# Laying the early pair products of a graph layer ahead of the last gather group, with 45 more behind the third group

## The chip, the cores and the metric

The kernel runs on one core of a Trainium2 chip. The metric is the device time of one execution in microseconds (us). Engines are called as in the profile: PE (matmul) and PEld (its weight load), DVE (vector), ACT (scalar), POOL (GpSimd, here mostly the issuer of row gathers) and SP (issues transfers).

## What is computed

Four graph attention layers over one graph of N = 3,327 nodes with 256 features, each followed by the residual and a layer norm. The adjacency is symmetric, about 1% full, with a full diagonal.

```python
x = layernorm(x + L0(x, adj))   # scores a.leaky(W_s x_i + W_t x_j), softmax over neighbours, sums of W_t x_j
x = layernorm(x + L1(x, adj))   # scores leaky(s1_i + s2_j) of h = W x, softmax over neighbours, sums of h_j
x = layernorm(x + L2(x, adj))   # scores s_i + s_j + b (no leaky), softmax, sums of h_j
x = layernorm(x + L3(x, adj))   # two layers like L1 with 4 heads of 64, elu after each
```

In layer 1 the weight of a neighbour can be written exp(s1_i + s2_j) or its 0.2-fold, whichever is larger in the exponent. Factors of the row cancel in the softmax, so the kernel forms e = max(rate_i, f_j) x adjacency and multiplies by rows that already carry their own exponential. A partial sum over some column tiles j can be stored and the rest added later; a column of exponentials carried with the features gives the denominator. This is what makes "early products" possible.

## The kernel before

The nodes are 26 tiles of 128 rows. Layer 0 is *sparse* (`sparse0`): the rows are handled in four groups of `SETS = (4, 7, 9, 6)` tiles. For each group a *search* (`neighbours`, scan with MAX8 at L589, sort L597/L599, ranks L688/L692) lists each row's neighbours; POOL writes the lists (`write_list`, L741) and reads them back in order of length (`read_lists`, L749). Then 237 *parts*, each of up to four neighbours of the 128 rows of a tile, are gathered by POOL with one indirect transfer a neighbour (L926, g<-table_d), eight steps ahead of their use, in 22 buffers. DVE scores a part (`largest` L946, `weighted` L952); when a tile has all its scores, `weights` takes maximum and exponentials (L985, L990), and `combine` scales the rows on ACT (L1028) and sums them on PE against an identity (L1031). `add_input` divides and adds the input into a tile with the tag "hs" of two buffers (L1052 to L1058), and `put_back` stores it through POOL (L1065). The last tile's later cuts are summed on DVE instead (`add_aside`, L1007/L1009). When a group is complete, `take` loads it back into h, and `finish_sums`, `finish_root` (POOL, L1105) and `finish` (DVE, L1114) norm it.

All of this is one order written out by hand: in each step q, the loop at the end of `sparse0` first does so many steps of the next search as are owed by a due time (`owed`), then everything entered for this step by `at_step`, then the gather for part q + 8 and the score of part q. Engines keep this order. Parts of the groups begin at steps 0, 39, 102 and 182, and the last part is step 236. POOL's puts and list writes stand in a list `between` that is worked off between gathers.

Into the steps of layer 0 some work of layer 1 is laid. `load_next` loads its weight and two attention vectors, `dots_next` multiplies them (L1142, in tiles with the tag "hs" too). For the 20 tiles of the first three groups (`EARLY = 20`), `turn_next` and `project_next` make the layer 1 features and store them in `feats_d`. For the first two groups (`KNOWN = 11` tiles) the products of row tiles 0 to 10 with column tiles 0 to 10 are done early, too: for each *pair* of a trio of row tiles and a column tile, SP loads adjacency and features (at_f, three buffers), ACT casts the adjacency and stores it for a later layer (`weigh_early`, L1217), DVE forms e (L1221), PE adds (`add_early`, L1234), and after the last pair of a trio ACT copies the sums and stores them in `part_d` (`keep_early`, L1242). The trios are [0,1,2], [3,4], [5,6,7], [8,9,10], so there are 44 pairs.

Layer 1 itself (`one_head`) then goes over blocks of row tiles in the order 11 to 14, 0 to 4, 5 to 10, 15 to 19, 20 to 25. PE holds one accumulator for each row tile of the block and runs over the column tiles j (L1845), DVE forming e for each (L1728). Blocks of tiles up to 10 begin at j = 11 (`first_of`, `skip`) and add the stored sums by identity products (L1854) at j = skip + `LATER` (4). The preparation of the block before for layer 2 (turn L1765, copy, project L1653, bias L1691, scale L1692) lies in a queue `pending`; `work_off` takes steps of it, in these blocks once per column tile from j = skip + 4 on, and after the last column tile the rest. The end of group 3 (`last_group`) is worked off at the start of layer 1 in the same manner. Layers 2 and 3 follow in the same dense form; they are untouched.

Of the kernel before, what the change touches and what calls it, by code (L numbers as in the profile page):

```python
# [8 lines left out]
F32 = mybir.dt.float32  # L9
BF16 = mybir.dt.bfloat16  # L10
I32 = mybir.dt.int32
# [8 lines left out]
P = 128  # L20
# [12 lines left out]
SETS = (4, 7, 9, 6)  # L33
# [10 lines left out]
ROW = 260  # L44
# [6 lines left out]
def gat_stack(  # L51
# [29 lines left out]
    nc = tc.nc  # L81
    n, dim = x.shape
# [15 lines left out]
    ident = const.tile([P, P], F32, name="ident")  # L98
# [10 lines left out]
    EARLY = sum(SETS[:-1])  # L109
# [11 lines left out]
    KNOWN = sum(SETS[:-2])  # L121
    blocks1 = []
    for lo, hi in ((0, KNOWN), (KNOWN, EARLY), (EARLY, nt)):
        count = -(-(hi - lo) // 6)
# [6 lines left out]
    part_d = dram.tile([KNOWN * P, dim + 1], F32, name="part_d")  # L131
# [154 lines left out]


    def sparse0(lost):
        GROUP, TURNS, LEAD, SPREAD = 4, 22, 8, 8
        starts = [sum(SETS[:s]) for s in range(len(SETS))]  # L290
        with ExitStack() as s0:
            find = s0.enter_context(tc.tile_pool(name="s_find", bufs=2))
            const0 = s0.enter_context(tc.tile_pool(name="s_const", bufs=1))
            io0 = s0.enter_context(tc.tile_pool(name="s_io", bufs=2))
# [767 lines left out]
            def put_back(s, t):  # L1062

                entry = held.pop((s, t))
                nc.gpsimd.indirect_dma_start(  # L1065
                    out=sums_d[s][:, :],
                    out_offset=bass.IndirectOffsetOnAxis(
                        ap=entry["lst"][:, KMAX : KMAX + 1], axis=0
                    ),
                    in_=entry["y"][:, :], in_offset=None,  # L1070
                )
# [55 lines left out]
            def load_next():  # L1127
                nc.sync.dma_start(w1[:, :, :dim], l1_w_t.rearrange("(c p) f -> p c f", p=P))
                for v in (l1_a[dim:], l1_a[:dim]):
                    t = find.tile([P, dim], F32, tag="minus", name="row1")  # L1130
                    nc.sync.dma_start(
                        t, bass.AP(tensor=v.tensor, offset=v.offset, ap=[[0, P], [1, dim]])
                    )
                    rows1.append(t)

            def early_bank():
                return ps0.tile([P, BANK], F32, tag="v", name="early", bufs=4)
# [44 lines left out]
                for block in blocks1 if block[-1] < KNOWN  # L1182
                for lo in range(block[0], block[-1] + 1, 3)
            ]
            pairs1 = [(trio, j) for trio in trios for j in range(KNOWN)]
            asked1, formed1, state1 = {}, {}, {}

            def ask_early(m):
                if m >= len(pairs1):
                    return  # L1190
                trio, j = pairs1[m]
                lo, w = trio[0] * P, len(trio) * P
                if j == 0:
                    b = [trio[0] in block for block in blocks1].index(True)
                    at0 = trio[0] - blocks1[b][0]
                    rate = find.tile([P, 3 * P], F32, tag="adj_b", name="rate1", bufs=3)
                    rows = rate1_d[b][at0 : at0 + len(trio), :].rearrange("s i -> (s i)")
                    nc.sync.dma_start(rate[:, :w], rows[None].to_broadcast([P, w]))
                    state1["next"] = rate
                t = find.tile([P, PIECE], I32, tag="adj_i", name="at_f", bufs=3)  # L1200
                f = t[:, BANK : BANK + dim + 2].bitcast(F32)
                copy_rows(nc.sync, t[:, :w], adj_t[j * P : (j + 1) * P, lo : lo + w])
                nc.sync.dma_start(f, feats_d[j * P : (j + 1) * P, :])
                asked1[m] = t, f

            def weigh_early(m):
                trio, j = pairs1[m]
                lo, w = trio[0] * P, len(trio) * P
                t, f = asked1[m]
                if j == 0:  # L1210
                    state1["rate"] = state1["next"]
                if m == 0:
                    state1["e"] = find.tile(
                        [P, max(SETS) * P], F32, tag="key_rows", name="e1", bufs=1
                    )
                at = find.tile([P, 3 * P], BF16, tag="cand", name="at1")
                nc.scalar.copy(at[:, :w], t[:, :w])  # L1217
                nc.scalar.dma_start(at_d[j * P : (j + 1) * P, lo : lo + w], at[:, :w])
                x = m % 3 * 3 * P
                e = formed1[m] = state1["e"][:, x : x + w]  # L1220
                nc.vector.scalar_tensor_tensor(  # L1221
                    e, state1["rate"][:, :w], f[:, dim + 1 : dim + 2], t[:, :w],
                    op0=ALU.max, op1=ALU.mult,
                )

            def add_early(m):
                if m < 0:
                    return
                trio, j = pairs1[m]
                e, (_, f) = formed1.pop(m), asked1.pop(m)  # L1230
                if j == 0:
                    state1["accs"] = [early_bank() for _ in trio]
                for s, acc in enumerate(state1["accs"]):
                    nc.tensor.matmul(  # L1234
                        acc[:, : dim + 1], e[:, s * P : (s + 1) * P], f[:, : dim + 1],
                        start=(j == 0), stop=(j == KNOWN - 1),
                    )

            def keep_early(m):
# [47 lines left out]
            def at_step(q, what, *args):  # L1287
                due.setdefault(q, []).append(lambda: what(*args))
# [17 lines left out]
            for q, key in ends.items():  # L1306
                count = len(cuts_of(seats[key]))
                if key[1] == 0:
                    at_step(q + 2, send_weights, key[0])
                    at_step(q + 3, take_weights, key[0])  # L1310
                    at_step(q + 4, combine_excess, key[0])
                for i in range(count):
                    at_step(q + 1 + i * SPREAD // max(count, SPREAD), combine, *key, i)
                at_step(q + 10, add_input, *key)
                at_step(q + 13, between.append, lambda key=key: put_back(*key))
                if key[1] == SETS[key[0]] - 1 and key[0] < len(SETS) - 1:
                    at_step(q + 21, take, key[0])
                    at_step(q + 27, finish_sums, key[0])
                    at_step(q + 33, finish_root, key[0])
                    at_step(q + 37, finish, key[0])  # L1320
            for s, q in begins.items():
                work, at = excess(s), max(q - 2, 0)
                for y in range(12):
                    at_step(at + y, go_on, work)
            at = begins[len(SETS) - 1] - 2 * KNOWN - 3
            at_step(at - 12, load_next)
            at_step(at - 6, dots_next, 0)
            at_step(at - 4, dots_next, 1)
            for s in range(len(SETS) - 1):
                for it in range(starts[s], starts[s] + SETS[s]):  # L1330
                    at_step(at, turn_next, it)
                    at_step(at + 2, project_next, it)
                    at += 2
                if s == len(SETS) - 3:
                    at = max(at, begins[len(SETS) - 1] + 38)
            at = begins[len(SETS) - 1] + 2
            at_step(at - 2, ask_early, 0)
            at_step(at - 1, ask_early, 1)
            for m, (trio, j) in enumerate(pairs1):
                at_step(at, add_early, m - 1)  # L1340
                if j == 0 and m:
                    at_step(at + 1, keep_early, m - 1)
                    at += 1
                at_step(at, weigh_early, m)
                at_step(at, ask_early, m + 2)
                at += 1
            at_step(at, add_early, len(pairs1) - 1)
            at_step(at + 1, keep_early, len(pairs1) - 1)
            def keep_targets(s):
                lo, hi = starts[s] * P, min(n, (starts[s] + SETS[s]) * P)  # L1350
                copy_rows(nc.sync, own_d[s][: hi - lo, AT_TGT:], table_d[1 + lo : 1 + hi, :])
# [5 lines left out]
            ahead, owed, steps = [], {}, 0  # L1357
            for s in range(1, len(SETS)):
                at = begins[s] - LEAD - 2
                at_step(at, read_lists, s)  # L1360
                at -= SETS[s] // 2 + 1
                for it in range(SETS[s]):
                    at_step(at, between.append, lambda s=s, it=it: write_list(s, it))
                ahead.append(neighbours(s))
                steps += steps_of(s)
                owed[at] = steps
# [227 lines left out]
    def layers(rs, early=0, rest=None):  # L1594
# [209 lines left out]
                work_off()  # L1804

        def first_of(layer, b):
            return KNOWN if early and layer is l1 and layer.blocks[b][-1] < KNOWN else 0

        def ask_parts(block):

# [10 lines left out]
        def one_head(layer, make, banks_next):  # L1821
# [7 lines left out]
            for turn_b, b in enumerate(layer.order):  # L1829
# [6 lines left out]
                for j in range(skip, nt):  # L1836
# [3 lines left out]
                    for s, it in enumerate(block):  # L1840
                        pn = rows_of(it)
                        for part in range(1 if layer.leaky else 3):
# [6 lines left out]
                                start=(j == skip and part == 0),  # L1849
                                stop=(j == nt - 1 and (layer.leaky or part == 2)),  # L1850
                            )
                    if skip and j == skip + LATER:
                        for acc, y in zip(accs, parts):
                            nc.tensor.matmul(  # L1854
                                acc[:, : dim + 1], ident, y, start=False, stop=False
                            )
# [448 lines left out]
```

## Time and profile before

| | us |
|---|---|
| three timed runs | 3,307.76, 3,314.23, 3,329.03 (median 3,314.23) |
| profiled execution | 2,906.56 |
| its span | 2,904.8 (mean granted PE clock 0.887) |
| PE busy in the span | 2,310.4 (80%) |
| DVE busy | 2,128.0 (73%) |
| ACT busy | 866.0 (30%) |
| POOL busy | 991.7 (34%) |

The profiled execution is shorter than the timed runs; numbers from it are compared with its own time. In the page, a row of slices gives an engine's busy share in tenths over 40 equal slices of the span. A row of a group reads: line, engine, operation, output<-input, shapes, count | busy us, mean ns of one | idle us before, and who ended it. A row of the waits reads: engine, tile, line <- what it waited for: us in total, times, longest. A row of the timeline reads: start in us, duration, engine, line, operation, tiles and count, and in brackets the wait before it and what ended it.

### The profile page before, as it was taken

To read this page: it belongs to the slowest core of one execution; us is meant where nothing else is said; L and a number is where in the kernel's file an instruction comes from. 1 tells how busy PE (TensorE), PEld (TensorE's weight loads), DVE (VectorE), ACT (ScalarE), POOL (GpSimd) and SP (SyncE) were. 2 spreads that over 40 slices of the span, in tenths; PEclk is the share of its full clock that TensorE was granted. 3 is DMA by queue.
4 is the path that set the end of the run, shared out by engine and by line. 5 is a ranking of instruction groups with operands and counts; after the bars stand their busy time and mean duration, and the time that the engine had idled before them with its cause. 6 is when DMAs were issued, how large, how long until landed. Compare 5 with 4: busy or idle time off the path is not lost.

```text
span 2904.8 us, 47707 instructions
## 1 busy us (share of the span) xinstructions
PE 2310.4 (80%) x16735; PEld 1545.7 (53%) x16764; DVE 2128.0 (73%) x5634; ACT 866.0 (30%) x2441; POOL 991.7 (34%) x1059
## 2 busy tenths in 40 slices
PE   6466657555552665767899999999999999999997
PEld 4234435433442444645778888863656667534332
DVE  7799799968872856655455421158999999899997
ACT  4145445443432533544344311111011110110111
POOL 2676777777777777772000000000000000000000
PEclk9577778777776887889999999999999999999998
DMA  7795665445544557765767533331222222212211
GB/s 245 204 271 146 184 190 156 140 141 148 161 115 109 126 162 196 199 177 159 219 179 202 169 93 111 105 90 45 78 80 62 75 80 64 71 43 63 60 45 49
DMA packets 207558, 378.52 MB, mean 130 GB/s; under 512 B 38410, under 2 KB 148080, under 8 KB 206288
## 3 DMA queue, kind: packets, MB, share of 16 engines
q1 hardware_dynamic: 119416, 186.29, 22.5%
q0 software_dynamic: 50768, 154.31, 19.3%
q10 hardware_dynamic: 37128, 34.79, 3.6%
q8 instruction: 137, 2.24, 0.3%
q14 instruction: 109, 0.89, 0.1%
HBM read 333.91 MB, written 47.67 MB: 131 GB/s over the span
## 4 chain that ended last, share of the span: by engine, by line
PE 53%; DVE 8%; POOL 6%; DMA 6%; issue 5%; ACT 2%; ACTq 0%; SPq 0%; DVEq 0%; POOLq 0%; another core or an unknown queue 0%
PE acc L1913 18%; PE acc L1845 14%; PE acc L1921 9%; PE acc L1031 7%; POOL g L926 5%; DVE e L1728 3%; DMA g<-table_d,lst 3%; PE misc L1653 3%; DMA at_d<-at 1%; DVE y L952 1%; ACT g L1028 1%; DMA at<-at_d 1%; DVE y L946 1%; PE early L1234 1%; PE misc L1765 0%
## 5 line engine op out<-in xcount | busy, mean ns | idle before, releaser
L926 POOL DMA_INDIRECT g<-table_d,lst x894 | 853.9, 955 | 275.8 <-issue 237.6
L1728 DVE SCALAR_TENSOR_TENSOR e<-rate,feat,at 128x896 f32<-128x896 f32 (+4 forms) x832 | 843.4, 1078 | 59.0 <-PE acc L1921 47.8
L1913 PE MATMUL acc<-e,feat 128*32 128x384 f32 (+2 forms) x6656 | 691.5, 514 | 2.8 <-DVE e L1728 1.4
L1031 PE MATMUL acc<-g,ident 128*128 128x256 f32 x1766 | 484.5, 430 | 70.7 <-ACT g L1028 47.1
L1913 PEld LDWEIGHTS acc<-e,feat 128*32 128x32 f32 x6656 | 307.1, 110 | 294.9 <-issue 157.4
L1031 PEld LDWEIGHTS acc<-g,ident 128*128 128x128 f32 x1766 | 378.9, 219 | 158.2 <-ACT g L1028 64.9
L1921 PE MATMUL acc<-e,feat 128*32 128x384 f32 (+3 forms) x3328 | 383.6, 512 | 0.0
L1028 ACT ACTIVATE g<-g,w 128x256 f32<-128x256 f32 x883 | 367.5, 495 | 15.1 <-ACT at L1217 10.6
L946 DVE TENSOR_TENSOR y<-g,minus_ps 128x1028 f32<-128x1028 f32 (+2 forms) x233 | 273.3, 1173 | 110.0 <-DMA g<-table_d,lst 100.4
L952 DVE SCALAR_TENSOR_TENSOR y<-y,a_ps 128x257 f32<-128x257 f32 x894 | 324.6, 418 | 15.7 <-PE a_ps L810 2.2
L1845 PE MATMUL acc<-feat,e 128*128 128x257 f32 (+1 forms) x1110 | 257.5, 388 | 15.8 <-DVE e L1728 14.6
L1845 PE MATMUL acc<-feat,at 128*128 128x257 bf16 (+2 forms) x2028 | 239.3, 275 | 8.2 <-DMA at<-at_d 7.6
L1845 PEld LDWEIGHTS acc<-feat,e 128*128 128x128 f32 (+1 forms) x1110 | 211.6, 194 | 50.9 <-DVE e L1728 15.3
L1921 PEld LDWEIGHTS acc<-e,feat 128*32 128x32 f32 (+1 forms) x3328 | 162.1, 110 | 131.0 <-issue 88.7
L1845 PEld LDWEIGHTS <-at 128*128 128x128 bf16 (+2 forms) x2028 | 199.6, 100 | 42.4 <-issue 4.7
L563 PE MATMUL v<-code,leads 65*128 65x512 bf16 (+1 forms) x182 | 79.7, 438 | 144.2 <-DVE cand L589 103.3
L589 DVE MAX8 cand<-v 128x8 f32<-128x104 f32 (+2 forms) x858 | 157.1, 258 | 1.1 <-PE v L566 1.1
L1728 DVE SCALAR_TENSOR_TENSOR e<-rate,feat,at_i 128x640 f32<-128x640 f32 (+4 forms) x108 | 95.9, 899 | 82.3 <-DMA at_i<-in_adj_t_dram 27.7
L1706 POOL DMA_DIRECT2D rate3b_d<-rate_rows x4 | 2.1, 520 | 450.2 <-ACT rate_rows L1705 450.2
L1031 PE MATMUL acc<-own_of,ident 128*128 128x256 f32 x52 | 28.6, 650 | 140.3 <-ACT own_of L1028 89.8
L2099 POOL TENSOR_TENSOR rstds<-rstds,minus_half 128x7 f32<-128x7 f32 (+1 forms) x4 | 7.6, 1906 | 381.9 <-DVE rstds L2098 381.9
L261 POOL TENSOR_TENSOR rstds<-rstds,minus_half 128x6 f32<-128x6 f32 (+3 forms) x9 | 12.4, 1381 | 357.8 <-DVE rstds L260 357.8
(259 smaller groups left out, 2055.7 us busy)
## 6 DMA issues: line engine op xcount, KB each, us to landing
adj_i<-in_adj_dram SPq DMA_DIRECT2D x75, 512.0 KB
at<-at_d SPq DMA_DIRECT2D x150, 224.0 KB
at<-at_d SPq DMA_DIRECT2D x75, 192.0 KB
at<-at_d SPq DMA_DIRECT2D x75, 191.8 KB
g<-table_d,lst POOLq DMA_INDIRECT x894, 3.1
at_i<-in_adj_t_dram SPq DMA_DIRECT2D x39, 320.0 KB
at_i<-in_adj_t_dram SPq DMA_DIRECT2D x25, 383.5 KB
at_i<-in_adj_t_dram SPq DMA_DIRECT2D x25, 256.0 KB
```

The source lines that it names most:

```text
L563: nc.tensor.matmul(v[:, :w], leads[:, b, :], code[:, :w], start=True, stop=False)
L589: nc.vector.max(spread[:, c0 + c, :], view(v[:, :w]))
L926: nc.gpsimd.indirect_dma_start(out=g[:, k - k0, :], out_offset=None, in_=table_d[:, :], in_offset=bass.IndirectOffsetOnAxis(ap=entry["lst" ...
L946: nc.vector.tensor_tensor(y, rows, minus_src[:, None, :].to_broadcast([P, m, dim + 1]), op=ALU.max)
L952: nc.vector.scalar_tensor_tensor(y, y, 1.0, a_ps[:, : dim + 1], op0=ALU.mult, op1=ALU.mult, accum_out=sc)
L1028: nc.scalar.activation(rows, rows, AF.Copy, scale=w[:, k : k + 1])
L1031: nc.tensor.matmul(dst, ident, rows, start=start, stop=stop)
L1653: nc.tensor.matmul(pacc[:pn, : dim + self.extra], ht[:, k, :pn], self.weight[:, k, :], start=(k == 0), stop=(k == kc - 1),)
L1728: nc.vector.scalar_tensor_tensor(e[:pn, : c1 - c0], self.rate[b][:pn, h_of, : c1 - c0], q, at[:pn, : c1 - c0], op0=ALU.max, op1=ALU.mult,)
L1845: nc.tensor.matmul(accs[s][:pn, : dim + 1], a[:pj, s * P : s * P + pn], f[:pj, : dim + 1], start=(j == skip and part == 0), stop=(j == nt ...
L1913: nc.tensor.matmul(accs[x][p][q : q + 32, : hi - lo], f[:pj, at0 : at0 + 32], es[at0 // hd][:pj, lo:hi], start=(j == 0), stop=(j == nt - 1),)
L1921: nc.tensor.matmul(accs[x][pairs][h_of * 32 : (h_of + 1) * 32, : hi - lo], f[:pj, dim + h_of : dim + h_of + 1].to_broadcast([pj, 32]), es[ ...
```

## The change

- The due time of the last search is set by `SOONER = 32`: at step 182 − 34 − 4 = 144, where it was 168; its lists are read at step 148, where it was 172. POOL's list writes for it come after gather 573 instead of 667.
- `load_next` moves from step 145 to 124, the dots from 151 and 153 to 130 and 132, the features of tiles 0 to 10 from steps 157–179 (one every second step) to 136–148 (one a step). The two attention rows are loaded into tiles with the tag "row", where it was "minus".
- The 44 early pairs are weighed at steps 150–197, where it was 184–230; their sums are kept at 162, 174, 186 and 198.
- The third group's last sums come sooner: `combine` spread over 6 steps, not 8, input added at +7, not +10, put back at +8, not +13, taken and normed at +18, 21, 23, 26, not +21, 27, 33, 37. This is step 199 to 207, where it was 202 to 218. Its nine tiles' features follow at steps 211–219, where it was 222–238.
- 18 more pairs, trios [0,1,2] and [3,4] with column tiles 11 to 19, are weighed at steps 222–240; they load the stored sums back (five tiles, on SP), add them by five identity products, and store them again. The change is described as 54 tile products of six tiles; in the source the block has five tiles (0 to 4), which gives 45.
- In layer 1, block 0 to 4 begins at j = 20 instead of 11. The stored sums are added one column tile sooner, at skip + 3.

The core of the diff:

```diff
-        GROUP, TURNS, LEAD, SPREAD = 4, 22, 8, 8
+        GROUP, TURNS, LEAD, SPREAD, SOONER = 4, 22, 8, 8, 32
...
-                    t = find.tile([P, dim], F32, tag="minus", name="row1")
+                    t = io0.tile([P, ROW], F32, tag="row", name="row1", bufs=3)[:, :dim]
...
-            pairs1 = [(trio, j) for trio in trios for j in range(KNOWN)]
+            runs1 = [(trio, range(KNOWN)) for trio in trios]
+            runs1 += [(trio, range(KNOWN, EARLY)) for trio in trios if trio[-1] in blocks1[0]]
+            pairs1 = [(trio, j, js) for trio, js in runs1 for j in js]
...
+                if j and j == js[0]:
+                    state1["sums"] = []
+                    t = find.tile([P, PIECE], I32, tag="adj_i", name="sums_f", bufs=3)
+                    for x, it in enumerate(trio):
+                        y = t[:, x * (dim + 1) : (x + 1) * (dim + 1)].bitcast(F32)
+                        nc.sync.dma_start(y, part_d[it * P : (it + 1) * P, :])
+                        state1["sums"].append(y)
...
+                if j and j == js[0]:
+                    for acc, y in zip(state1["accs"], state1.pop("sums")):
+                        nc.tensor.matmul(acc[:, : dim + 1], ident, y, start=True, stop=False)
...
+                near = key[0] == len(SETS) - 2
+                spread = 6 if near else SPREAD
...
-                at_step(q + 10, add_input, *key)
-                at_step(q + 13, between.append, lambda key=key: put_back(*key))
+                at_step(q + (7 if near else 10), add_input, *key)
+                at_step(q + (8 if near else 13), between.append, lambda key=key: put_back(*key))
...
+                    after = (18, 21, 23, 26) if near else (21, 27, 33, 37)
...
-            at = begins[len(SETS) - 1] - 2 * KNOWN - 3
+            at = begins[len(SETS) - 1] - SOONER - KNOWN - 3
...
-                    at += 2
+                    projected[it] = at + 2
+                    at += 1
...
-                    at = max(at, begins[len(SETS) - 1] + 38)
-            at = begins[len(SETS) - 1] + 2
+                    at = max(at, begins[len(SETS) - 1] + 27)
+            at = begins[len(SETS) - 1] - SOONER
...
+            lay_early(at, range(count))
+            lay_early(projected[EARLY - 1] + 3, range(count, len(pairs1)))
...
+                if s == len(SETS) - 1:
+                    at = min(at, begins[s] - SOONER - 2)
...
-            return KNOWN if early and layer is l1 and layer.blocks[b][-1] < KNOWN else 0
+            if not early or layer is not l1 or layer.blocks[b][-1] >= KNOWN:
+                return 0
+            return KNOWN if b else EARLY
...
-                    if skip and j == skip + LATER:
+                    if skip and j == skip + LATER - 1:
```

`lay_early` is the old loop over the pairs as a function: it asks for the loads of the first two pairs, then in each step adds the pair before, keeps the sums where a trio ends, weighs a pair and asks for the one two ahead.

## The prediction

> **What bounds the kernel now.** I read first the page's busy lines and slices, then a table of stages, then the costly groups, the waits of POOL, the groups around the early products by form, and last the timelines of the places that the change touches. The slices show two regimes:
>
> ```profile
> PE   6466657555552665767899999999999999999997
> ...
> POOL 2676777777777777772000000000000000000000
> ...
> L926 POOL DMA_INDIRECT g<-table_d,lst x894 | 853.9, 955 | 275.8 <-issue 237.6
> ```
>
> Until slice 18 of 40 (1,323 us) POOL issues the row gathers, L926; after it PE is full and POOL empty. By stage (columns as in the first line):
>
> ```profile
> core 0: us, PE busy (x) PEld busy (x) DVE busy (x) ACT busy (x) POOL busy (x), PEclk, DMA share, GB/s
> 60.00:1323.00 1263.00, 747.36 (x2764) 544.42 (x2788) 962.81 (x3832) 531.57 (x1421) 938.30 (x982) 0.76 0.59 165
> ...
> 1422.00:1465.00 43.00, 41.41 (x185) 35.03 (x186) 24.03 (x56) 14.53 (x30) 1.02 (x1) 0.96 0.66 197
> ```
>
> In the first stage POOL is 74% busy and its rest is its own issue, 237.6 us over 775 gathers, 0.3 us each: (853.9 + 275.8) / 894 = 1.26 us per gather, about 5.3 us per step of up to four. PE (59%) and ACT (42%) have room, DVE (76%) some. What POOL waits for:
>
> ```profile
> POOL g L926 <- issue: 237.6, 775, 2.0
> POOL g L926 <- PE acc L1031: 18.0, 53, 2.2
> POOL lists_d L741 <- DVE ranks_i L692: 9.1, 1, 9.1
> ```
>
> So the sums cost it 18 us in all, and once, at an earlier search, the list writer stood 9.1 us because the ranks were late. Block 0 of layer 1, 1,422 to 1,465, has PE busy 41.4 of 43 us. The change takes PE work out of this block and lays it where POOL sets the pace.
>
> **What the skill says.** "Perfetto Trace Analysis", Optimization Strategy: a kernel can have regimes with different most-contended engines, and interleaving them may help. The stages agree. "TensorE: Matmul & The Clock Gate", Part 1: PE's default is throttled and activity releases it; here the granted clock is 0.76 in the sparse stage and 0.96 in block 0, so a product laid early costs more there: harmless while PE has room. "DMA: Bandwidth & Descriptors", Issuing engines are not separate DMA queues: transfers issued by SP, ACT and POOL share the same 16 engines. More loads could thus slow the gathers, but the share here is 0.59.
>
> **The change, part by part.**
>
> *(a) Block 0, the only work removed from the PE stage.* Its five tiles start at column tile 20, not 11: 9 x 5 = 45 products go, not 54, since the block has five tiles (0 to 4). A product is two passes:
>
> ```profile
> 1435.99 2.33 PE L1854 MATMUL acc<-parts,ident 128*128 128x257 f32 x10
> ...
> 1438.16 8.83 PE L1845 MATMUL acc<-feat,e 128*128 128x257 f32 x40
> ```
>
> 8.83 / 40 = 0.22 us, so 90 passes give 19.6–19.9 us. Not all of it arrives. The block also carries the preparation of the four tiles before it (11 to 14) for layer 2, a chain of turn, copy, project, bias and scale through one bank:
>
> ```profile
> 1463.10 0.38 PE L1765 MATMUL misc<-ident,h 128*128 128x128 f32 x2
> ...
> 1464.01 1.14 PE L1653 MATMUL misc<-l2w,turned 128*128 128x257 f32 x4 [0.53 <-ACT turned L1768]
> ...
> 1465.27 0.41 DVE L1691 TENSOR_TENSOR v<-misc,bias 128x256 f32<-128x256 f32 x1
> ```
>
> From 1463.10 to about 1466.1 one tile takes 3.0 us, 1.3 to 1.5 of it on PE. Now the steps of this chain lie between the products; with six column tiles only two (24, 25) work off a step, and the rest runs back to back after them. Block after: 60 passes x 0.2175 = 13.0, parts 2.2, four chains x 3.0 = 12, remaining waits as now 2.8; sum 30 of 42.8, so −12.8. I take −12. Bounds: −19.6 if the chain stays hidden, −9 if each tile exposes 4 us.
>
> *(b) The 45 products laid early* come after the third group's projections, at steps 222 to 240 of 237 gather steps: nine pairs of three tiles, nine of two, five partial sums reloaded and added, stored again. DVE: 9 x 0.615 + 9 x 0.482 = 9.9 us; PE 90 passes x 68.6 / 242 = 25.5 us and ten identity passes; ACT casts 9 x 0.505 + 9 x 0.399 + 5 copies x 0.373 = 10 us; in about 110 us where POOL issues. These rows:
>
> ```profile
> L1234 PE MATMUL early<-at_f,e 128*128 128x257 f32 x242 | 68.6, 423 | 32.4 <-DVE e L1221 31.9 <-ACT ht L1154 0.5
> ...
> L1221 DVE SCALAR_TENSOR_TENSOR e<-rate,at_f 128x384 f32<-128x384 f32 x33 | 20.3, 615 | 27.3 <-DMA at_f<-feats_d 21.9 <-PE acc L1031 3.7 <-PE early L1234 1.7
> L1217 ACT CAST at<-at_f 128x384 bf16<-128x384 int32 x33 | 16.7, 505 | 25.6 <-DMA at_f<-in_adj_t_dram 23.6 <-ACT part L1242 0.8 <-DMA at_d<-at 0.8
> ```
>
> Covered by POOL's issue: nothing. Each pair waits for its load at_f, on DVE and ACT; queued behind it are DVE's scores and ACT's scaled rows, which free POOL's buffers; POOL runs 8 steps (42 us) ahead on 22 buffers, and DVE's 27.3 us of such waits in 33 operations cost POOL nothing in the kernel before. SP carries 18 more feature and adjacency loads (three buffers) and five sums; block 0 loads nine fewer adjacency blocks.
>
> *(c) The tail* from the last gather (1,322.4) to the last store of sums, which frees layer 1's last column tiles:
>
> ```profile
> 1337.44 0.33 ACT L990 ACTIVATE w<-sc,top 128x28 f32<-128x28 f32 x1
> ...
> 1344.61 5.17 DVE L1009 SCALAR_TENSOR_TENSOR aside<-g,w,aside 128x256 f32<-128x256 f32 x10
> ...
> 1351.73 0.96 POOL L1065 DMA_INDIRECT sums_d<-hs,lst  x1 [6.14 <-DVE counts L1392]
> ```
>
> The weights (L990) are 7.5 us behind their maximum (1,329.9) because ACT is serving projections and a keep. In the changed order no projection lies here (they end at step 219), but four or five two-tile pairs do; a cast with its load wait is 0.4 + 0.4 us, and the last at_f lands about 1,341. I take −2 us; −6 if ACT is free, +4 if the pairs come in ahead of the sums.
>
> *(d) The first 44 pairs, projections of tiles 0 to 10, the column dots and the last search come earlier.* Same instructions, 34 to 21 steps sooner; POOL's gathers keep their order, only its six list writes (L741, 0.99 us each) come after gather 573 instead of 667. No saving: the ordinary due time of the search was step 168, but it ended near 150 by the common pace; now 144. What moves is a DVE stall. The dots' tile shares its two buffers with the sums `hs`, so each dots waits for a put_back that POOL issues later:
>
> ```profile
> 891.89 1.01 POOL L1065 DMA_INDIRECT sums_d<-hs,lst  x1 [0.30 <-issue]
> ...
> 894.39 0.42 DVE L1142 TENSOR_TENSOR dots<-w,row 128x256 f32<-128x256 f32 x1 [7.71 <-DMA sums_d<-hs,lst]
> ...
> 939.73 1.00 POOL L1065 DMA_INDIRECT sums_d<-hs,lst  x1 [0.30 <-issue]
> ...
> 942.21 0.43 DVE L1142 TENSOR_TENSOR dots<-w,row 128x256 f32<-128x256 f32 x1 [40.14 <-DMA sums_d<-hs,lst]
> ```
>
> Those two stores are POOL's steps 146 and 155: 47.84 / 9 = 5.3 us per step. In the new order the second tile of the dots at step 130 needs the store that POOL issues in its step 131, about 891.9 − 15 x 5.3 = 812 us; DVE arrives there six steps sooner, 779, and stands until 816: 37 us, in place of the 40 and 8 us above. Here they cost nothing, as POOL lives on its lead. But now the last search lies behind it in DVE's order. POOL needs the ranks at its step 144, 883 us, so DVE has 883 − 816 = 67 us for the rest of it. By counts in the changed order and this trace's durations that is 54 score operations x 0.36 (L952 took 26.6 us for 73 between 780 and 885), 16 x 1.22 (L946), 28 MAX8 x 0.19, sort 4.3, ranks 6.7, other 8.4: 63.6 us. I take no stall of POOL, with a margin of only 3 us; below nothing it can't go, as no gather leaves.
>
> *(e) The third group's sums*: combine spread over 6, not 8 steps, input and store 3 to 5 steps sooner, take to finish by step 207, not 218. POOL's wait on the sums (18.0 us in 53 times) could move by a few us: zero, ±5.
>
> *(f) The attention rows in another tile tag, parts added one column tile sooner*: SP's wait for the old tag goes, SP is not on the path; zero.
>
> Sum: −12 − 2 + 0 = −14 on the profiled execution, 2,906.6 to 2,892.5 us. The timed runs (median 3,314) are 14% longer than that; spread over the PE stage, the −12 become about −14: forecast **3,298 us**.
>
> **Rivals.** (1) *The full gain*: chain hidden (−19.6), tail −6 to −8, stretched by the same 1.14: about −30 to −35, 3,280. For it: a column tile is ten passes, 2.2 us, and nearly covers a 3 us chain. Against: only two of them work off a step. (2) *Given back*: 4 us per chain exposed, tail +4: −5, about 3,309. For: at_f waits of 22–24 us in the groups above. (3) *Slower: the last search is late.* POOL stands at L741 for the ranks, as it once did for 9.1 us; every gather behind it waits. The point: the DVE needs more than 67 us after its stall at the dots; each microsecond more is one on the whole. If each of the some 14 steps exposes 3 us of PE or load latency, 63.6 + 42 − 67 = 39 us, less the 14: +25, about 3,340. For: the margin is a twentieth of the work. Against: DVE has stood 40 us without loss to POOL. (4) *It doesn't do what it says*: 45 products instead of 54, true by the block's size, and in the forecast.
>
> **How the numbers follow.** Forecast 0.50, rival 1 0.25, rival 2 0.12, rival 3 0.13. About 1% (33 us) is what a measurement of this kernel can tell from no change. Faster by over 1% needs rival 1's upper half or a sparse stage that runs shorter: 0.28. Slower by over 1%, hence rival 3 in full: 0.10. Within: 0.62. The range 3,262 to 3,328 leaves out the worst of rival 3 and a gain beyond rival 1.
>
> **What would show it.** Right: 1020 passes at L1845 (now 1110), 332 passes of early products (now 242); block 0 about 30 us; a DVE wait of 30–40 us at L1142 near 780–816 with no POOL wait at L741; POOL's last gather within 5 us of 1,322. Wrong: POOL idle at L741 of over 10 us (rival 3), block 0 near 23 us (rival 1), the last store of sums after 1,355 (rival 2).

## The result, and the profile after

The changed kernel took 3,357.97 us (median of four, 3,348.17 to 3,371.36) against 3,318.66 for the kernel before (four, 3,307.76 to 3,329.03): a ratio of 1.0112, 95% interval 1.0064 to 1.0161, slower by 39 us. The forecast was 3,298, in a range to 3,328.

One thing must be known to read the numbers: in this comparison and in one of the experiments the kernel before ran near 3,320 to 3,330, in the others near 2,906, as in the profile shown of it, so times are set against each other within one comparison, and across comparisons only as ratios to a kernel before of the same length.

The profile of the changed kernel is of an execution at 3,348. The rows of its page that answer to those of before:

```profile
PE   7156365544545544455467899999999999999997
...
POOL 2724645566655564536650000000000000000000
...
L926 POOL DMA_INDIRECT g<-table_d,lst x894 | 854.0, 955 | 390.1 <-issue 260.5
```

The answer for line 926 alone gives the shortest, median and longest gather in ns, then the start of the first and the last:

```profile
L926 POOL DMA_INDIRECT g<-table_d,lst x894: 943/950/1317, 86.6 to 1737.9; - x179
```

A gather takes the same 0.95 us, but POOL's digits are mostly 4 to 6 where they were 7, and the last one starts at 1,737.9, not 1,322.4. By stage (gathers; to the last store of sums; to block 0; block 0):

```profile
core 0: us, PE busy (x) PEld busy (x) DVE busy (x) ACT busy (x) POOL busy (x), PEclk, DMA share, GB/s
60.00:1738.00 1678.00, 821.32 (x2794) 579.88 (x2792) 948.10 (x3756) 527.65 (x1415) 939.93 (x984) 0.69 0.46 126
1738.00:1805.00 67.00, 47.79 (x198) 39.41 (x198) 47.07 (x149) 34.46 (x87) 3.58 (x4) 0.90 0.40 109
1805.00:1877.00 72.00, 56.69 (x246) 46.05 (x246) 29.18 (x61) 23.74 (x59) 5.10 (x7) 0.93 0.81 242
1877.00:1909.00 32.00, 25.15 (x94) 19.05 (x95) 22.89 (x68) 9.98 (x23) 2.19 (x2) 0.82 0.59 182
```

The dense part is as it was and block 0 is short, 32 us; all of the extra length lies in the gather stage and its tail (67 us, where it was 29). No engine is full in the gather stage: DVE is busy for 948 of 1,678 us, POOL for 940. POOL's waits up to the last store say what it stood for:

```profile
POOL g L926 <- issue: 260.5, 826, 2.8
POOL sums_d L1065 <- DVE hs L1056: 246.3, 21, 30.1
POOL g L926 <- PE acc L1031: 67.9, 29, 12.1
...
POOL lists_d L741 <- DVE ranks_i L692: 16.8, 2, 9.1
```

In the profile of the kernel before, at 2,906, the waits ahead of the same 26 stores were these, so that all but the last two went out within 0.3 us:

```profile
  DVE aside L1007: 20.0, 1
  DVE counts L1392: 6.1, 1
  issue: 6.1, 20
```

Not all of the new row is the change's, however. The first two groups' stores stand where they stood before, and they wait, too: 80 us ahead of their eleven stores in this profile, against 137 us ahead of the third group's nine. So a part of these waits goes with the longer execution. The first store of all, then five of the third group's, with the wait ahead of each:

```profile
303.94 1.01 POOL L1065 DMA_INDIRECT sums_d<-hs,lst  x1 [12.19 <-DVE hs L1056]
...
1264.87 1.14 POOL L1065 DMA_INDIRECT sums_d<-hs,lst  x1 [11.94 <-DVE hs L1056]
1331.11 1.01 POOL L1065 DMA_INDIRECT sums_d<-hs,lst  x1 [26.04 <-DVE hs L1056]
1388.99 1.14 POOL L1065 DMA_INDIRECT sums_d<-hs,lst  x1 [17.99 <-DVE hs L1056]
1445.65 1.14 POOL L1065 DMA_INDIRECT sums_d<-hs,lst  x1 [18.83 <-DVE hs L1056]
1508.02 1.14 POOL L1065 DMA_INDIRECT sums_d<-hs,lst  x1 [27.41 <-DVE hs L1056]
```

The five are 102 us in which not one gather leaves. The timeline around the second of them:

```profile
1281.25 1.46 PE L1246 MATMUL early<-at_f,e 128*128 128x257 f32 x6
...
1304.13 0.95 POOL L926 DMA_INDIRECT g<-table_d,lst  x1 [0.30 <-issue]
1305.01 0.33 SPq L146 DMA_DIRECT2D at_f<-in_adj_t_dram  x1
...
1307.96 0.48 DVE L1230 SCALAR_TENSOR_TENSOR e<-rate,at_f 128x256 f32<-128x256 f32 x1 [26.72 <-DMA at_f<-feats_d]
...
1315.44 6.34 PE L1031 MATMUL acc<-g,ident 128*128 128x256 f32 x16 [31.00 <-ACT g L1028]
...
1330.41 0.42 DVE L1056 TENSOR_TENSOR hs<-hs,bt_rows 128x256 f32<-128x256 f32 x1
...
1331.11 1.01 POOL L1065 DMA_INDIRECT sums_d<-hs,lst  x1 [26.04 <-DVE hs L1056]
1332.43 0.97 POOL L926 DMA_INDIRECT g<-table_d,lst  x1 [0.30 <-issue]
```

From 1,284 to 1,305 PE, DVE and ACT do nothing, and SP issues nothing, while POOL gathers. The early pair's load leaves at 1,305, DVE's e follows at 1,308, PE has stood for 31 us when it begins the tile's sums, the finished sums come at 1,330.8, and POOL, which reached the store at 1,305, goes on gathering only at 1,332. What held SP and ACT in that gap the trace doesn't show: it holds some 25,100 of the semaphore records by which a wait is traced to its end, where a profile of the same kernel at 2,903 holds some 41,600.

### The profile page after: what moved, and what is told of

It is laid out like the page before. It is cut to its first block, busy times and chain, and to the rows that moved or that the text cites. A ratio compares the mean times of both kernels' runs of the same rounds, so it can differ in the third digit from the quotient of the medians.

```text
span 3346.3 us, 47923 instructions
## 1 busy us (share of the span) xinstructions
PE 2396.2 (72%) x16774; PEld 1589.3 (47%) x16774; DVE 2137.3 (64%) x5643; ACT 872.5 (26%) x2455; POOL 994.3 (30%) x1059
## 5 line engine op out<-in xcount | busy, mean ns | idle before, releaser
L1031 PE MATMUL acc<-g,ident 128*128 128x256 f32 x1766 | 535.3, 458 | 328.5 <-issue 167.0
L1031 PEld LDWEIGHTS acc<-g,ident 128*128 128x128 f32 x1766 | 405.2, 235 | 440.0 <-issue 188.2
L1873 PE MATMUL acc<-feat,e 128*128 128x257 f32 (+1 forms) x1020 | 235.5, 388 | 18.3 <-DMA at_i<-in_adj_t_dram 11.3
L1873 PEld LDWEIGHTS acc<-feat,e 128*128 128x128 f32 (+1 forms) x1020 | 195.4, 194 | 49.9 <-DVE e L1754 22.2
L589 DVE MAX8 cand<-v 128x8 f32<-128x104 f32 (+2 forms) x858 | 165.0, 261 | 59.3 <-issue 42.5
L1230 DVE SCALAR_TENSOR_TENSOR e<-rate,at_f 128x384 f32<-128x384 f32 (+1 forms) x62 | 35.5, 572 | 166.5 <-DMA at_f<-feats_d 99.8
L1754 DVE SCALAR_TENSOR_TENSOR e<-rate,feat,at_i 128x640 f32<-128x640 f32 (+6 forms) x99 | 88.1, 901 | 71.8 <-DMA at_i<-in_adj_t_dram 29.3
```

The costliest lines, as they stand in the source:

```text
L589: nc.vector.max(spread[:, c0 + c, :], view(v[:, :w]))
L1031: nc.tensor.matmul(dst, ident, rows, start=start, stop=stop)
L1754: nc.vector.scalar_tensor_tensor(e[:pn, : c1 - c0], self.rate[b][:pn, h_of, : c1 - c0], q, at[:pn, : c1 - c0], op0=ALU.max, op1=ALU.mult,)
L1873: nc.tensor.matmul(accs[s][:pn, : dim + 1], a[:pj, s * P : s * P + pn], f[:pj, : dim + 1], start=(j == skip and part == 0), stop=(j == nt ...
```

## The experiments

**Where the length lies.** The kernel before again, and the changed one again.

> The kernel before, unchanged, for a profile of an execution at the length of the timed runs (about 3,315 us); the profile shown of it ended at 2,907. All theories expect a ratio of 1.00 (0.995 to 1.005). They differ in where the 408 us between the two lie. If the dense layers are slowed by a lower clock, as the prediction assumed, block 0 of layer 1 takes about 49 us instead of 42.8 and the last gather ends near 1,330. If the gather stage is the slow part, as it is in the profile of the changed kernel (last gather at 1,738), the last gather ends near 1,710 and block 0 still takes about 43 us.

> The changed kernel, unchanged, where the kernel before runs in 2,906 us. First reading (the loss of 39 us lies in the changed program itself): a ratio of about 1.011, 2,938 us, with waits of POOL for the third group's sums as in the profile at 3,348. Second reading (the loss belongs to executions in which DVE, ACT and PE are held up in the gather stage, so that POOL's stores meet sums that aren't ready): no such waits, the gathers end within 5 us of 1,322, block 0 takes about 30 us, and the ratio is 0.995 (2,892), as the prediction's sum for the profiled execution has it, or nearer to 1.00 if the pairs hold up the last sums.

Measured: 2,904.80 (before 2,906.24), ratio 0.9998 (0.9987 to 1.0009); and the changed kernel 2,902.99 (before 2,906.14), 0.9987 (0.9978 to 0.9996). So the kernel before was met here only at 2,906, and its last gather at 1,326.8 says nothing on where its own 3,319 went; the first expectation stays open for it. For the changed kernel both lengths are there, and they differ in the gather stage and its tail. The second reading of the other expectation is the one that held, but for the end of the gathers, at 1,332.7 where it was to lie within 5 us of 1,322. The stages of before, then of the changed kernel, cut at the same events as above:

```profile
60.00:1327.00 1267.00, 747.66 (x2771) 543.32 (x2795) 964.13 (x3842) 532.43 (x1423) 937.83 (x983) 0.76 0.59 165
1327.00:1356.00 29.00, 23.29 (x94) 18.58 (x95) 14.29 (x40) 17.19 (x52) 2.74 (x4) 0.90 0.43 100
1356.00:1423.00 67.00, 54.19 (x242) 42.97 (x240) 28.21 (x61) 23.74 (x59) 5.12 (x7) 1.00 0.81 237
1423.00:1468.00 45.00, 41.98 (x186) 35.36 (x187) 24.35 (x56) 14.73 (x30) 1.02 (x1) 0.96 0.65 195
```

```profile
60.00:1333.00 1273.00, 780.08 (x2897) 575.90 (x2923) 971.01 (x3851) 550.37 (x1471) 939.07 (x983) 0.76 0.61 170
1333.00:1361.00 28.00, 15.12 (x62) 12.33 (x60) 14.80 (x44) 10.46 (x27) 3.13 (x4) 0.83 0.32 81
1361.00:1433.00 72.00, 56.63 (x246) 45.99 (x246) 29.23 (x62) 23.74 (x59) 5.24 (x7) 0.92 0.81 241
1433.00:1465.00 32.00, 25.54 (x94) 19.36 (x95) 22.63 (x68) 10.24 (x24) 2.19 (x2) 0.83 0.62 189
```

Block 0 gives 12 us here (its first products start at 1,423.3 and 1,433.2, the next block's at 1,467.8 and 1,465.1: 44.5 to 32.0). The gathers take 7 us more from first to last (84.1 to 1,332.7, against 85.6 to 1,326.8), and 5 us go between the last store and block 0 (72 for 67; 70.5 in the other profile of before). No store of the third group waits over 0.3 us. This profile of the kernel before is of the longest of its 14 executions, 2,916 us, and has 7 us more behind block 0 than the one at 2,907; the two are therefore compared by stage, not by their sums.

**The parts, where the kernel before runs at 2,906.** The third group's sums at their old distances:

```diff
-                near = key[0] == len(SETS) - 2
+                near = False
...
-                    at = max(at, begins[len(SETS) - 1] + 27)
+                    at = max(at, begins[len(SETS) - 1] + 38)
```

> The changed kernel with the third group's sums at their old distances (spread 8, input at +10, store at +13, take to finish at +21, 27, 33, 37), its features and the 18 later pairs following 11 steps later. Theory N (the stores of the third group now stand one step behind their sums in POOL's order, and POOL waits for them: 26, 18, 19 and 27 us at 1,331 to 1,508 in the changed profile): the waits of these stores fall below 5 us each and the gathers end 60 to 100 us sooner, but the pairs now lie behind the last gather; net 20 to 60 us faster than the changed kernel, ratio to before 0.99 to 1.005. Theory T (the 18 later pairs hold up the last sums after the last gather): slower than the changed kernel by 10 to 30 us, ratio 1.015 to 1.02, since more of them come late. Theory S (the earlier search is late): no change, 1.011.

2,924.60, ratio 1.0071 (1.0055 to 1.0087): 18 us over the kernel before where the changed kernel is 3 under it, so by these ratios 21 us slower than the changed one. The last store comes 38 us after the last gather instead of 28, since more pairs lie there. Theory T's sign, and near its size, but what it shows is that with the later pairs in place the sooner sums pay at this length: in the changed kernel no store of the third group waited in the first place.

Without the 18 later pairs:

```diff
-            runs1 += [(trio, range(KNOWN, EARLY)) for trio in trios if trio[-1] in blocks1[0]]
...
-            lay_early(projected[EARLY - 1] + 3, range(count, len(pairs1)))
...
-            return KNOWN if b else EARLY
+            return KNOWN
```

> The changed kernel without the 18 later pairs: block 0 of layer 1 begins at column tile 11 again, all else as changed. Theory T: the stretch from the last gather to the last store of sums falls from 66 us to about 30, block 0 takes 12 us more; net about 24 us faster than the changed kernel, ratio to before about 1.004. Theory N: this part is a gain, so it is about 12 us slower than the changed kernel, 1.015. Theory S: as N, 1.015.

2,907.48, 1.0004 (0.9995 to 1.0013): against the changed kernel's 0.9987 the later pairs are worth 5 us, not 12. The tail is 23 us (1,328.9 to 1,352.0) without them and 28 with them.

Only the search sooner (`SOONER`, the `min` at its due time, in the kernel before):

> The kernel before with the last search due at step 144 instead of 168 (and its lists written and read sooner), nothing else of the change. Theory S: POOL waits for the ranks of the last search (7.7 us in the changed profile), or the gathers lose pace through a denser search; ratio to before 1.005 to 1.011. Theories N and T: nothing, 0.997 to 1.003.

2,910.28, 1.0016 (1.0006 to 1.0025); from first gather to last 1,241.7 us, as before (1,241.2). A cost of about 4 us, whose place stays open: the profile is of the shortest execution, 2,901.7, and can't show it. Two of the 22 executions, at 5,884 and 11,748 us, aren't in the ratio; their cause isn't known.

Neither the later pairs nor the sooner sums (both diffs above):

> The changed kernel without the 18 later pairs and without the sooner sums of the third group: only the search, the features of tiles 0 to 10 and the 44 pairs come earlier, and the later features at one a step. If parts add up: the distance from this kernel to the one without the later pairs alone (1.0004) is what the sooner sums are worth by themselves, expected nothing within 0.2%, as they only serve to let the pairs begin; ratio 0.999 to 1.003. If POOL's stores one step behind the sums cost it something even here, this kernel is 0.2 to 0.4% faster than that one.

2,907.47, 1.0006 (0.9997 to 1.0015): equal to the one without the pairs, so the sooner sums alone are worth nothing that shows at this length. Its gathers already take 1,247.7 us, and 1,246.0 without the later pairs alone, where the search alone left them at 1,241.7: so the longer gathers come with the earlier features and pairs, not with the later pairs. These are single profiles; the kernel with the dots apart, below, takes the time of the changed one with 1,244.5, so the 7 us are better read as 3 to 7.

**The stores and the dots.** Stores at +13 with sums at +7:

```diff
-                at_step(q + (8 if near else 13), between.append, lambda key=key: put_back(*key))
+                at_step(q + 13, between.append, lambda key=key: put_back(*key))
```

> The changed kernel with the third group's stores at +13 again, five steps later, its sums still at +7. Where POOL waited for these sums (the profile at 3,348), this takes 100 us of waits away and should be 20 to 60 us faster than the changed kernel; where POOL doesn't wait for them (executions near 2,906), nothing: within 0.1% of the changed kernel.

2,914.55, 1.0029 (1.0020 to 1.0038): 12 us slower than the changed kernel, where nothing was expected at this length. The dots and the list writer, first of the changed kernel, then of this one:

```profile
826.46 0.42 DVE L1142 TENSOR_TENSOR dots<-w,row 128x256 f32<-128x256 f32 x1 [27.46 <-DMA sums_d<-hs,lst]
```

```profile
851.52 0.42 DVE L1142 TENSOR_TENSOR dots<-w,row 128x256 f32<-128x256 f32 x1 [49.35 <-DMA sums_d<-hs,lst]
...
901.55 1.01 POOL L741 DMA_INDIRECT lists_d<-payload,ranks_i  x1 [8.65 <-DVE ranks_i L692]
```

The dots wait for a store that now comes five steps later: 49 us for 27. The search behind them is late, and POOL stands 8.65 us for the ranks. This is rival 3, at the place and by the mechanism that it names; in the changed kernel the writer waits 0.3 us there. The dots in the buffers of the scores take the wait away:

```diff
-                    t = io0.tile([P, dim], F32, tag="hs", name="dots1")
+                    t = io0.tile([P, GROUP, dim + 1], F32, tag="y0", name="dots1")[:, 0, :dim]
```

> The changed kernel with the tile of the column dots in the buffers of the scores instead of the sums, so that DVE's dots no longer wait for a store of POOL. The prediction has this wait at about 37 us near 780 to 816 us, with the last search behind it. If the search's margin is used up there (rival 3), POOL's wait for the ranks goes and the kernel is faster than the changed one by what it was; if DVE's wait is covered, as the forecast has it: the wait at the dots is gone and the time is the same within 0.1%.

2,903.84, 0.9992 (0.9981 to 1.0003): the wait at the dots is gone and the time is the same, so 27 us of it were covered.

**A stage slowed on purpose.** DVE fills a score tile ahead of chosen steps; nothing else changes.

```diff
+            def hold():
+                y = io0.tile([P, GROUP, dim + 1], F32, tag="y0", name="hold")
+                for _ in range(16):
+                    nc.vector.memset(y, 0.0)
+
+            for q in range(100, 233, 12):
+                at_step(q, hold)
```

> The kernel before with DVE held up on purpose: 16 fills of a score tile (about 1 us each, from the fill of 512 elements at 0.485 us) ahead of every 12th step from 100 to 232, twelve times, some 186 us of DVE in all. It takes nothing out. It stands for executions like the one at 3,348, in which DVE, ACT and PE stand still for some 20 us at a time while POOL gathers on. All theories: POOL's stores at +13 meet finished sums, so POOL waits little for sums and what the holds cost is what doesn't fit in DVE's idle time; 0 to 60 us over the kernel before (ratio 1.00 to 1.02).

> The changed kernel with the same holds. Theory N (a store one step behind its sums takes POOL's lead away, so that DVE's standstills reach POOL): POOL waits for the third group's sums by 5 to 15 us a store, and this kernel is 20 to 60 us slower than the held kernel before, though the changed one without holds is 3 us faster than the unheld one. Theory S (the search's margin is 3 us by the prediction's sum): POOL waits for the ranks by 10 us or more, the same sign. No theory of the prediction's forecast survives if it is slower; if the difference stays at -3 us, neither explains the loss at 3,348.

> The changed kernel with the holds and the third group's stores at +13. Theory N: the waits for the third group's sums go, and it is 20 to 50 us faster than the held changed kernel. Theory S: it stays as slow or gets slower, since the dots then wait five steps longer for a store (53 us instead of 28 in the unheld pair) and the ranks come later still (8.7 us of POOL's waits there without any hold).

> The changed kernel with the holds and without the 18 later pairs. If the pairs behind the third group hold up the last sums under holds (theory T): the stretch from the last gather to the last store is over 10 us shorter than in the held changed kernel and the whole is about equal or faster in spite of 12 us more in block 0. If not: 8 to 12 us slower.

With the kernel before at 2,908.78: held before 2,976.29, held changed 2,960.23, with stores at +13 2,979.54, without the later pairs 2,960.45. The changed kernel stays the faster by 16 us (its tail is 69 us, that of the held kernel before 84), and the later stores cost 19: the opposite of theory N. Twelve holds don't make the loss, though it was expected of them. They do show rival 3 once more: with the stores at +13 POOL waits 27.14 us for the ranks (4.85 with the stores at +8). Without the later pairs the tail falls from 69 to 54 us and the whole is equal, as theory T has it.

Then 52 holds: `range(11)` fills ahead of every step of `range(30, 237, 4)`, in a comparison in which the kernel before ran at 3,332.47:

> The kernel before with 11 fills of a score tile ahead of every 4th step from 30 to 234: 52 holds of DVE of some 13 us (a fill took 0.92 us and 1.19 with its gap in the first held kernels), 680 us in all, of which about 300 fit in DVE's idle time. So DVE and what hangs on it set the pace of the gather stage, as in the executions of the first comparison (3,314), and POOL waits. Expected: 3,230 to 3,330, ratio 1.11 to 1.15, under every theory.

> The changed kernel with these 52 holds. Theory W (where POOL is not the pace, the pairs laid early are no longer free: DVE, ACT and PE pay for them in a stage that they bound, 10 us of DVE, 10 of ACT and 25 of PE, and the pairs hold up the sums of the last tiles after the last gather): 10 to 50 us slower than the slowed kernel before, as it was at 3,314 against 3,358. Theory N (stores one step behind their sums): the same sign and size, with POOL's waits for the third group's sums in the profile, over 10 us a store. If it is equal to the slowed kernel before or faster, standstills of DVE alone are not what made the changed kernel lose.

> The changed kernel with the 52 holds and the third group's stores at +13. Theory N: 20 to 50 us faster than the slowed changed kernel. Theory W: within 10 us of it, or slower by the dots' longer wait.

> The changed kernel with the 52 holds, without the 18 later pairs. Theory W: 10 to 30 us faster than the slowed changed kernel, in spite of 12 us more in block 0, with a shorter stretch from the last gather to the last store. Theory N: 8 to 12 us slower than it.

| slowed kernel | us | ratio to the kernel before | first gather to last |
|---|---|---|---|
| before | 3,692.65 | 1.1066 (1.1030 to 1.1103) | 1,951 |
| changed | 3,741.71 | 1.1203 (1.1162 to 1.1244) | 2,004 |
| changed, stores at +13 | 3,703.92 | 1.1107 (1.1070 to 1.1143) | 1,961 |
| changed, without later pairs | 3,740.75 | 1.1211 (1.1174 to 1.1247) | 2,016 |

The slowed kernel before took 3,693 us where 3,230 to 3,330 was expected, as the kernel before ran at 3,332 here; its ratio is just under the low end of 1.11. Here the changed kernel loses 49 us to the kernel before, and moving nine stores by five steps gives 38 of them back, as theory N has it. Taking the later pairs away gives nothing, which is neither theory's figure: the tail falls from 115 to 92 us, but the gathers take 12 us more. The last of the third group's nine stores, in the slowed kernel before, in the changed one and in the one with stores at +13:

```profile
1780.15 1.13 POOL L1065 DMA_INDIRECT sums_d<-hs,lst  x1 [16.84 <-DVE hs L1056]
```

```profile
1823.49 1.14 POOL L1065 DMA_INDIRECT sums_d<-hs,lst  x1 [40.45 <-DVE hs L1056]
```

```profile
1784.72 1.01 POOL L1065 DMA_INDIRECT sums_d<-hs,lst  x1 [0.30 <-issue]
```

Ahead of all nine the waits are 122, 220 and 16 us. So the stores waited in the slowed kernel before, too, three steps behind their sums; one step behind they wait 98 us more, and six steps behind nearly nothing. POOL's waits for the sums of all groups and for buffers up to 2,120 us, of the slowed kernel before, of the changed one and of the one with stores at +13:

```profile
POOL sums_d L1065 <- DVE hs L1056: 292.1, 18, 52.8
...
POOL g L926 <- PE acc L1031: 141.0, 27, 24.8
```

```profile
POOL sums_d L1065 <- DVE hs L1056: 361.7, 19, 40.5
...
POOL g L926 <- PE acc L1031: 133.5, 19, 35.5
```

```profile
POOL g L926 <- PE acc L1031: 249.9, 35, 45.8
...
POOL sums_d L1065 <- DVE hs L1056: 201.1, 13, 54.9
```

With the stores at +13 the third group's waits fall by 204 us (the rows show less, as one wait of 55 us lies behind 2,120 in the changed kernel alone); 116 us come back as waits for free buffers and 21 as waits for ranks, and the gathers take 43 us less from first to last (2,004 to 1,961). A likely reading, not tested by itself: a POOL that isn't stopped at the store gathers on until its 22 buffers are full, and has more in hand when DVE comes back. Rival 3 has a share as well: the writer of the last search's lists waits 17.9 us in the slowed changed kernel and 0.3 in the slowed kernel before.

**A version with both.** Stores at +13 and the dots apart:

> The changed kernel with two edits: the third group's stores at +13 again, and the column dots in the buffers of the scores, so that the later stores don't hold DVE's dots (and with them the last search) as they did in the kernel with the stores alone (1.003). No holds. Where the kernel before runs near 2,906: 0.998 to 0.999, as the changed kernel. Where it runs near 3,320: theory N has it free of the changed kernel's loss, ratio 0.990 to 1.001; if the stores aren't the cause without holds, it stays at 1.008 to 1.012.

> The same kernel as the one before it, for an execution at the length of the comparison on record, should this be one: theory N then expects 0.990 to 1.001 to the kernel before, where the changed kernel had 1.011. If it runs near 2,906 again, it only repeats 0.998 to 0.999 and says nothing new on the cause.

2,901.92, 0.9984 (0.9976 to 0.9992), and 2,901.66, 0.9990 (0.9980 to 1.0001). At this length it is 5 us below the kernel before and can't be told from the changed one (0.9987); the 12 us of the stores at +13 went with the dots' wait, which settles their cause. In neither comparison did the kernel before run near 3,320, so that this version keeps clear of the loss there isn't shown.

## Why the prediction was wrong

Two steps failed: the one from the profile to the timed runs, and step (e), which priced the third group's sooner sums without the wait of their stores.

- *The sum for the profiled execution*: −14 predicted; −3 to −4 measured where both kernels run near 2,906 (2,902.99 against 2,906.14, ratio 0.9987). Step (a) held: block 0 from 42.8 or 44.5 to 32.0 us, −12 taken, and 45 products went, not 54 (1,020 passes at the product's line of layer 1, 332 early passes). Step (c) held in sum: the tail went from 29 to 28. Its parts were each larger: no projections in it −6, the pairs +5. What failed there is the term "covered by POOL's issue: nothing" of (b) and "no saving", at no cost, of (d): the gathers took 3 to 7 us more, which came with the earlier features and pairs, and some 2 to 5 us more lie between the last store and block 0, where the last pairs run until 1,355.9 and layer 1 begins at 1,367.3.
- *The step from there to the timed runs*, "spread over the PE stage, the −12 become about −14": wrong. In the changed kernel's execution at 3,348 the dense part isn't stretched at all; block 0 takes the same 32 us. The gather stage is. The prediction had no row that showed where the 14% lay, and so it left POOL's issue in charge of a stage where in this execution POOL itself waits.
- *Step (e), "POOL's wait on the sums [...] could move by a few us: zero, ±5"*: the step that failed on the sign, as far as the runs show. It costed the sooner sums by a wait of POOL for PE, and didn't cost the store's own wait: a store one step behind its sum, with every later gather queued behind it on POOL. Where DVE, ACT and PE keep their lead it is nothing, as forecast; at 3,348 it is 137 us of waits ahead of nine stores, 102 of them at five. How much of that a kernel with the old distances would wait at this length was not measured. In the slowed kernels the stores one step behind wait 98 us more than those of the kernel before, and putting them six steps behind (the old distance was three) gives back 38 of the 49 us. For the comparison on record, without holds, it is argued from the same waits, not shown. The rest of the loss, and what makes executions of both kernels longer, stay open.
- *Rival 3* was near in time (3,340) and right in mechanism, but not the cause on record: at 3,348 the writer of the last search's lists waits 7.7 us, and the loss is 39. The dots' wait was put at 37 us and is 27, which costs nothing; a wait of 49 cost 8.7 in ranks, so DVE can stand for about 41 us there. That is the prediction's 37 and its margin of 3 together: the size of the search was right, the stall was shorter.
- *Rival 1* fell: the chain isn't hidden. *Rival 2* gave the right size (−5) for the wrong place.
- The range ended at 3,328, short even of rival 3's own 3,340, since the loss was given 0.13 in all.

## What to carry to other kernels

A wait put on an in-order engine is priced by what stands behind it, not by how ready its input was in one profile: a store that follows its producer by one step can turn a standstill of the producer into one of the engine that sets the pace, as with 52 holds here, though not with twelve. Leave such stores where the lead was, and check which later work waits for the buffer that they free. When the timed runs are longer than the profiled one, don't scale its stages: the stage that grows may be another one, with another engine in charge.

## What the runs showed of the hardware

The kernel before ran in two lengths 14% apart, near 2,906 and near 3,320 to 3,332 us, and the changed kernel in 2,903 and 3,358. Among the timed executions of the kernel before in one comparison the length didn't change. The experiments near 2,906 ran on chips 1, 2, 9 and 14 and the 52 holds on chip 7; for the comparison on record, and for the profile of the kernel before that is shown with it, the chip isn't noted. So the length may belong to the chip: no run here separates the two.

In the changed kernel's two profiles (2,902.7 and 3,346.3 us) the 894 gathers have the same median (0.950 us) and block 0 the same 32 us, but the gather stage takes 1,248.6 and 1,651.3 us from its first to its last, with a mean granted clock of 0.76 and 0.69. PE, DVE and ACT stand still together in both, but more often in the longer one: counted in the traces between the first gather and the last, 3 times for over 5 us (50 us in all, the longest 27 us at the dots) and 15 times (165 us, the longest 23.5). No row of the profile names the cause.
